# Ranking the first half's router logits token tile by token tile in a hand-planned instruction list

## The chip, the cores and the metric

The kernel runs on one core of one Trainium2 chip. The metric is the device time of one execution in microseconds (us), as the median of several runs. A profile of one execution goes with it: when each instruction ran on each engine, what it waited for, and the clock that was granted to the matrix engine.

The engines are called by their short names: PE multiplies matrices (PEld is its loading of weights, which overlaps the multiplications), DVE is the vector engine, ACT the scalar engine, POOL the general-purpose one and SP the one that issues most DMAs. PE writes to PSUM, which has eight banks; the other engines read results from there.

## The reference, cut to what matters

`x` is 16 batches of 112 tokens of 256 numbers (1,792 tokens), `ctx` is 16 batches of 375. One cross-attention layer and one mixture-of-experts layer follow each other, all in float32:

```python
h = layernorm(x)
q = h @ Wq + bq;  k = ctx @ Wk + bk;  v = ctx @ Wv + bv
x = x + softmax(q @ k.T / 16) @ v                       # per batch

h = layernorm(x)
router_probs = softmax(h @ w_router)                    # 256 -> 8 experts
gate_weights = softmax((h @ w_gating) / 0.1)
expert_out[e] = (silu(h @ w_gate[e]) * (h @ w_up[e])) @ w_down[e]   # 256 -> 1024 -> 256
cw = router_probs * gate_weights
cw = cw / (sum(cw) + 1e-9)
x = x + sum_e expert_out[e] * cw[e]
```

The router logits are the products `h @ w_router` and `h @ w_gating` together: 256 rows to 16 columns.

## The kernel before, in words

The 16 batches make two halves of eight (896 tokens, seven token tiles of 128). The work has two parts.

**The front** does the attention of all 16 batches, the second layer norm, both halves' router logits and the preparation of the first experts' weights. Its instructions are not in program order. Each step is registered with `op(engine, cost, pri, emit, reads, writes, new)`: an engine, a cost that the author wrote down, a rank `pri`, what it reads and writes, and new buffers that it needs. Then `Line.run` (lines 64 to 140) plays the list through with those costs: whenever an engine is free in this play, it takes, of the steps that are ready by then, the one with the lowest rank (line 119). The order that comes out is the order in which each engine gets its instructions. On the chip every engine then works through its own queue in that order and waits wherever something is not ready.

PSUM banks are given out in the same play. A step that opens a result takes one of the eight banks, and the bank is free again when the last step that reads the result is done.

The ranks follow the batch number. For batch `b` the steps on PE are:

| step, name in the profile | line | rank |
|---|---|---|
| two transposes of the context, `ps_cT` (three instructions each) | 1062 | b + 0.1 |
| scores, `ps_sc` | 1074 | b + 0.6 |
| transpose of the softmax, `ps_pp` | 1095 | b |
| softmax times context, `ps_aa` | 1108 | b - 0.4 |
| projection, `ps_po` | 1123 | b |
| transpose of the normalised result, `ps_xx` | 1170 | b - 0.5 |

Between them stand, for each group of four batches, the transposes and projections of the queries (`ps_xT`, line 999, and `ps_qk`, line 1016). After `ps_xx` a copy on ACT or DVE (line 745) puts the batch's columns into `x1T`, which is the input of the router and of the experts.

`route(h)` registers the router of half `h`. `logits(j)` does token tile `j`: two products of a 128 x 128 block of `x1T` with 16 columns, which the profile lists as four instructions of 128 x 16 into `ps_lg` (line 1203). All seven tiles write to one PSUM bank: tile 0 opens it, and each tile is registered as coming after the one before. Tile `j` covers tokens 128 j to 128 j + 127 and so reads two batches of 112 tokens, `b0` and `b1`, which are j and j + 1. One copy on ACT (line 1214) takes all seven tiles out of the bank; the softmax of the router follows on DVE and ACT. For half 0 that chain has no hurry: its last steps have rank 8.7 + 12. The half's splits into high and low parts (lines 297 and 300) do not read the logits.

**The experts** follow: 64 steps of products of the same shape (line 456), with the down projections (line 424) between them, in an order written out in the program. They take the time from about 110 us to the end.

Of the kernel before, what the change touches and what calls it, by code (L numbers as in the profile page):

```python
# [30 lines left out]
class Line:  # L31
# [13 lines left out]
    def op(self, eng, cost, pri, emit, reads=(), writes=(), new=(), waits=(), kb=0, port=False, lands=0.0):  # L45

        n = len(self.ops)
        if not isinstance(eng, tuple):
            eng, cost, go = (eng,), (cost,), emit
            emit = lambda e: go()  # L50
        deps = set()
        for k in reads:
            deps.update(self.writers[k])
        for k in waits:
            deps.update(self.uses[k])
        writes = tuple(writes) + tuple(x[1] for x in new)
        for k in tuple(reads) + writes:
            self.uses.setdefault(k, []).append(n)
        for k in writes:
            self.writers.setdefault(k, []).append(n)  # L60
        self.ops.append((eng, cost, pri, emit, deps, tuple(new), kb, port or eng == ("POOL",), lands))
        return n
# [81 lines left out]
def kernel(  # L144
# [249 lines left out]
    for q in range(E * NJ):  # L394
        e, j = divmod(q, NJ)
# [344 lines left out]
    op = line.op  # L740
# [10 lines left out]
    def bank(key, shape):  # L751

        if key not in banks_of:
            name = "_".join(str(x) for x in key)
            banks_of[key] = psum(line.home[key], f"ps_{name}")
        return shaped(banks_of[key], shape)
# [438 lines left out]
    def route(h):  # L1195

        key = ("lg", h)
        pri = (8.7, 21)[h]
        lg = lgs[h]

        def logits(j):
            for k in range(KC):
                nc.tensor.matmul(  # L1203
                    bank(key, [P, NTT, 2 * E])[:, j, :], x1T[h][:, k, j * P : (j + 1) * P], wr[:, k, :],
                    start=(k == 0), stop=(k == KC - 1),
                )

        for j in range(NTT):
            b0, b1 = j * P // TQ, (j * P + P - 1) // TQ
            op("PE", 0.46, pri, lambda j=j: logits(j),  # L1210
               reads=["wr"] + [("x1T", h * HB + b) for b in range(b0, b1 + 1)] + ([key] if j else []),
               writes=((key,) if j else ()), new=(() if j else (("bank", key, *((("D0", "D1", "D3"),) if h else ())),)))
        op("ACT", 0.26, (pri, 32)[h],
           lambda: nc.scalar.copy(lg, bank(key, [P, NTT, 2 * E]).rearrange("p j (s e) -> p j s e", s=2)),
           reads=(key,), writes=(("l", h),))

        def shift():
            nc.vector.reduce_max(lmx, lg, axis=AX.X)
            nc.vector.tensor_sub(lg, lg, lmx.unsqueeze(3).to_broadcast([P, NTT, 2, E]))

        def shifted(*after):
            op("DVE", 0.9, pri, shift, reads=[("l", h), *after], writes=(("ls", h),))


        def exps():
            nc.scalar.activation(lg[:, :, 0, :], lg[:, :, 0, :], AF.Exp)
            nc.scalar.activation(lg[:, :, 1, :], lg[:, :, 1, :], AF.Exp, scale=10.0)

        if h:
            later_shift.append(shifted)  # L1230
        else:
            shifted()
            op("ACT", 0.5, pri, exps, reads=(("ls", h),), writes=(("le", h), "exp"))

        def sums():
            nc.vector.reduce_sum(lmx, lg, axis=AX.X)
            nc.vector.reciprocal(lmx, lmx)

        def shares():
            nc.vector.tensor_mul(lg, lg, lmx.unsqueeze(3).to_broadcast([P, NTT, 2, E]))  # L1240
            nc.vector.tensor_mul(lpr, lg[:, :, 0, :], lg[:, :, 1, :])

        def rest():
            nc.vector.reduce_sum(lps, lpr, axis=AX.X)
            nc.vector.tensor_scalar_add(lps, lps, 1e-9)
            nc.vector.reciprocal(lps, lps)

        def weights():
            nc.vector.tensor_mul(
                cw[:, h * NTT : (h + 1) * NTT, :], lpr, lps.unsqueeze(2).to_broadcast([P, NTT, E])  # L1250
            )

        if h:
            tail.extend((exps, sums, shares, rest, weights))
            return
        op("DVE", 0.5, pri + 12, sums, reads=(("le", h),), writes=(("w1", h),))
        op("DVE", 0.55, pri + 12, shares, reads=(("w1", h),), writes=(("w2", h),))
        op("DVE", 0.6, pri + 12, rest, reads=(("w2", h),), writes=(("w3", h),))
        op("DVE", 0.3, pri + 12, weights, reads=(("w3", h),), writes=(("cw", h),))
# [5 lines left out]
    early = lambda h: [("x1T", h * HB + b) for b in range(HB // 2)]  # L1265
    late = lambda h: [("x1T", h * HB + b) for b in range(HB // 2, HB)]
    route(0)
    for h in range(NH):
        for i in (X_A11, X_A12):
# [5 lines left out]
    for i in (X_S2, X_S1, X_S3, X_A22, X_S4):  # L1275
        split(0, i, 10.5, *late(0), *([("sx", i)] if i != X_A22 else []))
    route(1)


# [6 lines left out]
    for k in range(EARLY):  # L1286
        pri = 9.5 + k
# [155 lines left out]
```

## Time and profile before

| what | value |
|---|---|
| device time, median of 3 runs | 958.62 us |
| the three runs | 958.07, 958.62, 959.26 us |
| span of the profiled execution, first to last instruction | 958.0 us |
| PE busy in that span | 952.4 us, 99% |
| mean granted PE clock, core 0 | 0.998 |
| the front, to the end of `ps_second` | 0 to about 109.7 us |
| the logits of half 0, first to last matmul | 61.36 to 65.61 us |
| the logits of half 1 | 97.13 to 108.97 us |

Of the profiled execution the page gives the span alone; the timed runs lie 0.1 to 1.3 us above it, and that is taken as what lies around the span together with the spread of the runs.

How to read it: the page lists the busy time of each engine and slices of the span; the chain of waits follows the work that ended last back to the start and names in order of time what it consisted of; the windows view gives busy time, instruction counts and the granted PE clock (1.00 is full) for any stretch. A matmul's end is modelled, so PE can read as busy while it works slowly.

### The profile page before, as it was taken

How to read it: one execution, taken by the hardware profiler on the slowest of the kernel's cores; microseconds unless marked ns; L12 is line 12 of the kernel's file. 1: busy time of each engine (PE TensorE's matmuls, PEld its weight loads, DVE VectorE, ACT ScalarE, POOL GpSimd, SP SyncE). 2: the span in 40 equal slices, each digit the busy share in tenths (PEclk: the TensorE clock that was granted, in tenths of full speed). 3: DMA queues.
4: the chain of work that ended last, by engine and by line, in shares of the span. 5: the costliest groups of instructions: out<-in, count | busy, mean ns of one | idle time of the engine just before them, and what ended most of it. 6: DMA issues, size and time to landing. Idle time of an engine off the chain costs nothing.

```text
span 958.0 us, 16137 instructions
## 1 busy us (share of the span) xinstructions
PE 952.4 (99%) x6076; PEld 896.6 (94%) x6076; DVE 656.1 (68%) x1303; ACT 608.8 (64%) x1236; POOL 377.4 (39%) x481
## 2 busy tenths in 40 slices
PE   9999999999999999999999999999999999999998
PEld 6898999999999999999999999999999999999998
DVE  6878687777576666666575757666666767566675
ACT  5767776666666665666656666666666666666553
POOL 3437973344324433344244332543244431544000
PEclk9999999999999999999999999999999999999999
DMA  9621101011101110011101110111001110100001
GB/s 243 183 58 43 59 23 34 23 34 45 34 12 34 34 45 23 22 36 34 34 23 34 34 34 23 34 34 34 23 23 34 44 34 12 34 23 12 23 17 39
DMA packets 36481, 38.78 MB, mean 40 GB/s; under 512 B 3554, under 2 KB 34404, under 8 KB 36404
## 3 DMA queue, kind: packets, MB, share of 16 engines
q1 hardware_dynamic: 35856, 37.50, 13.2%
q8 instruction: 47, 0.77, 0.3%
q10 hardware_dynamic: 548, 0.27, 0.1%
q14 instruction: 30, 0.25, 0.1%
HBM read 34.08 MB, written 1.84 MB: 37 GB/s over the span
## 4 chain that ended last, share of the span: by engine, by line
PE 98%; DVE 1%; ACT 1%; issue 0%; DVEq 0%; ACTq 0%
PE pd L424 32%; PE pC L456 16%; PE pE L456 16%; PE pA L456 16%; PE pB L456 8%; PE ps_aa L1108 2%; PE ps_sc L1074 2%; PE ps_cT L1062 1%; PE ps_po L1123 1%; PE ps_qk L1016 1%; PE ps_lg L1203 1%; PE ps_pp L1095 1%; PE ps_idle L822 1%; PE ps_xx L1170 0%; PE ps_xT L999 0%; DVE hlo L599 0%
## 5 line engine op out<-in xcount | busy, mean ns | idle before, releaser
L424 PE MATMUL pd<-wd,hhi 128*128 128x256 f32 x1792 | 311.2, 277 | 0.0
L424 PEld LDWEIGHTS pd<-wd,hhi 128*128 128x128 f32 x1792 | 275.8, 188 | 1.9
L424 PE MATMUL pd<-wd,hlo 128*128 128x256 f32 x896 | 248.6, 277 | 0.4 <-DVE hlo L599 0.3
L456 PE MATMUL pC<-xs_hi,w 128*128 128x448 f32 x508 | 185.0, 364 | 0.1
L456 PE MATMUL pE<-xs_hi,w 128*128 128x448 f32 x508 | 184.4, 363 | 0.0
L456 PE MATMUL pA<-xs_hi,w 128*128 128x448 f32 x504 | 183.3, 364 | 0.0
L359 POOL TENSOR_TENSOR w<-raw,w 128x384 fp32r<-128x384 f32 x64 | 78.4, 1225 | 266.0 <-ACT w L349 266.0
L424 PEld LDWEIGHTS pd<-wd,hlo 128*128 128x128 f32 x896 | 168.4, 188 | 0.8 <-DVE hlo L599 0.8
L653 ACT COPY pB<-pA 128x448 f32<-128x448 f32 x122 | 63.8, 523 | 104.0 <-PE pA L456 104.0
L368 POOL TENSOR_TENSOR wd<-rawd,wd 128x512 fp32r<-128x512 f32 x32 | 41.9, 1308 | 182.8 <-ACT wd L366 182.8
L456 PEld LDWEIGHTS pC<-xs_hi,w 128*128 128x128 f32 x508 | 95.3, 188 | 10.9 <-DVE s_90c L678 0.4
L456 PEld LDWEIGHTS pE<-xs_hi,w 128*128 128x128 f32 x508 | 95.4, 188 | 6.6
L456 PEld LDWEIGHTS pA<-xs_hi,w 128*128 128x128 f32 x504 | 94.6, 188 | 5.5
L663 ACT COPY pE<-pB 128x448 f32<-128x448 f32 x122 | 63.1, 517 | 54.2 <-DVE s_6s L530 0.8
L456 PE MATMUL pC<-xs_lo,w 128*128 128x448 f32 x254 | 91.9, 362 | 0.0
L456 PE MATMUL pE<-xs_lo,w 128*128 128x448 f32 x254 | 91.5, 360 | 0.0
L456 PE MATMUL pB<-xs_hi,w 128*128 128x448 f32 x252 | 91.4, 363 | 0.0
L456 PE MATMUL pA<-xs_lo,w 128*128 128x448 f32 x252 | 90.7, 360 | 0.0
L359 POOL TENSOR_TENSOR w<-tt,w 128x512 fp32r<-128x512 f32 x64 | 88.4, 1381 | 0.1
L456 PEld LDWEIGHTS pE<-xs_lo,w 128*128 128x128 f32 x254 | 47.6, 187 | 3.5
L456 PEld LDWEIGHTS pB<-xs_hi,w 128*128 128x128 f32 x252 | 47.3, 188 | 3.1
L456 PEld LDWEIGHTS pC<-xs_lo,w 128*128 128x128 f32 x254 | 47.6, 187 | 2.5
(1456 smaller groups left out, 1786.2 us busy)
## 6 DMA issues: line engine op xcount, KB each, us to landing
raw<-in_L_ffn_w_gate_dram SPq DMA_DIRECT2D x32, 256.0 KB, 2.6
raw<-in_L_ffn_w_up_dram SPq DMA_DIRECT2D x32, 256.0 KB, 2.6
rawd<-in_L_ffn_w_down_dram SPq DMA_DIRECT2D x32, 256.0 KB, 2.6
ctx<-in_ctx_dram SPq DMA_DIRECT2D x13, 336.0 KB
out_dram<-acc SPq DMA_DIRECT2D x6, 256.0 KB, 3.7
wide<-in_ctx_dram SPq DMA_DIRECT2D x3, 336.0 KB, 6.7
wide<-in_x_dram SPq DMA_DIRECT2D x2, 448.0 KB
ctx<-in_ctx_dram SPq DMA_DIRECT2D x13, 39.0 KB
```

The costliest lines, as they stand in the source:

```text
L359: nc.gpsimd.tensor_sub(wts[k][1][:, d], w, f(wts[k][0][:, d]))
L368: nc.gpsimd.tensor_sub(wds[q][1], rawds[q], f(wds[q][0]))
L424: nc.tensor.matmul(pd, hs[a][:, t * P : (t + 1) * P], wds[q][w][:, fi, :], start=(opening and s == 0), stop=(last and s == 2), skip_group_ ...
L456: nc.tensor.matmul(ps, w_[w][:, wi, :], (xs_hi, xs_lo)[a][h][xi], start=(start and s == 0), stop=(stop and s == 2), skip_group_check=True,)
L653: nc.scalar.copy(pb, pa)
L663: nc.scalar.copy(pe, pb)
L822: nc.tensor.matmul(bank(("idle", k), [P, 512]), zero[:, :P], zero, start=True, stop=True)
L1016: nc.tensor.matmul(bank(("qk", g, m, 0), [P, GT]), m_b[k][a][:, m * P : (m + 1) * P], xnT_b[k][w], start=(k == 0 and s == 0), stop=(k == K ...
L1062: nc.tensor.transpose(bank(("cT", b, k), [P, TK])[:, c * KT : (c + 1) * KT], ct()[:, c, k * P : (k + 1) * P], ident[:KT, :KT],)
L1074: nc.tensor.matmul(bank(("sc", b), [TQ, TK]), own(qk_b[k], ("qk", g, k))[:, i * TQ : (i + 1) * TQ], ctT(k), start=(k == 0), stop=(k == KC ...
L1095: nc.tensor.transpose(bank(("pp", b), [KT, NK, TQ])[:, c, :], p()[:, c * KT : (c + 1) * KT], ident[:TQ, :TQ])
L1108: nc.tensor.matmul(bank(("aa", b), [P, KC, TQ])[:, k, :], ct()[:, c, k * P : (k + 1) * P], pT()[:, c, :], start=(c == 0), stop=(c == NK - 1),)
```

## The change

The rank of the seven logits steps of half 0 was 8.7 for all. It becomes 6.5 + 0.5 b1, with b1 = j + 1: 7.0, 7.5, 8.0, 8.5, 9.0, 9.5 and 10.0 for tiles 0 to 6. The second half's logits keep rank 21, and the copy, the softmax and the weights after the logits keep their ranks (8.7 and 20.7). No instruction is added or removed; the list's play gives another order.

```diff
         for j in range(NTT):
             b0, b1 = j * P // TQ, (j * P + P - 1) // TQ
-            op("PE", 0.46, pri, lambda j=j: logits(j),
+            op("PE", 0.46, pri if h else 6.5 + 0.5 * b1, lambda j=j: logits(j),
                reads=["wr"] + [("x1T", h * HB + b) for b in range(b0, b1 + 1)] + ([key] if j else []),
                writes=((key,) if j else ()), new=(() if j else (("bank", key, *((("D0", "D1", "D3"),) if h else ())),)))
```

## The prediction

> **What bounds the kernel now.** I read the page first, then the chain of waits through the front in order of time, then the windows view around the logits with its clock column, then the same windows for the tile `ps_lg` alone, and last PEld's waits. The page:
>
> ```profile
> span 958.0 us, 16137 instructions
> PE 952.4 (99%) x6076; PEld 896.6 (94%) x6076; DVE 656.1 (68%) x1303; ACT 608.8 (64%) x1236; POOL 377.4 (39%) x481
> PE 98%; DVE 1%; ACT 1%; issue 0%; DVEq 0%; ACTq 0%
> ```
>
> PE bounds it: 5.6 us of the span are without a matmul, and the chain is PE's for 98%. The change removes no work. So it can gain only where PE is busy yet slow, and lose only where PE comes to wait. The chain of waits around the logits (start, length, what):
>
> ```profile
> 59.95 1.41 PE ps_aa L1108 x12
> 61.36 0.81 PE ps_lg L1203 x8
> 62.17 0.24 PE ps_xx L1170 x2
> 62.41 0.37 PE ps_lg L1203 x4
> 62.78 0.79 PE ps_po L1123 x6
> 63.57 0.35 PE ps_lg L1203 x4
> 63.92 0.24 PE ps_xx L1170 x2
> 64.16 1.46 PE ps_lg L1203 x12
> 65.61 3.11 PE ps_cT L1062 x15
> 68.72 1.26 PE ps_sc L1074 x4
> ```
>
> Here is such a place. Fifteen transposes take 3.11 us; earlier in the same chain twelve take 1.29 (40.46 to 41.76), so fifteen should take 1.61. The windows view says why. Its columns are stretch, length, busy time of PE, PEld, DVE, ACT and POOL with counts, then the PE clock and the DMA's share:
>
> ```profile
> 61.67:65.08 3.41, 3.41 (x34) 3.41 (x33) 2.68 (x10) 2.22 (x6) 0.55 (x1) 1.00 0.12 36
> 65.08:68.49 3.41, 3.41 (x19) 3.41 (x19) 2.23 (x11) 2.11 (x7) 2.63 (x3) 0.50 0.12 34
> 68.49:71.90 3.41, 3.41 (x18) 2.22 (x17) 2.67 (x7) 2.87 (x9) 1.50 (x2) 1.00 0.00 0
> ```
>
> For 3.41 us the clock was at 0.50, and PE counts as busy throughout. What stood just ahead of it shows in the same view for `ps_lg` alone (columns PE, PEld, ACT, clock):
>
> ```profile
> 61.67:65.08 3.41, 2.63 (x24) 2.63 (x23) 0.00 (x0) 1.00 0.12 36
> 65.08:68.49 3.41, 0.54 (x4) 0.43 (x3) 0.25 (x1) 0.50 0.12 34
> 95.80:99.21 3.41, 0.98 (x8) 0.97 (x8) 0.00 (x0) 1.00 0.09 24
> 99.21:102.63 3.42, 0.51 (x4) 0.53 (x4) 0.00 (x0) 1.00 0.04 10
> 102.63:106.04 3.41, 0.96 (x8) 0.97 (x8) 0.00 (x0) 1.00 0.35 111
> 106.04:109.45 3.41, 1.19 (x8) 1.04 (x8) 0.25 (x1) 1.00 0.42 115
> ```
>
> Logits filled 2.63 us of the stretch before the fall, and a logits matmul streams 16 columns where a transpose streams 125. Half 1 has the same 28 instructions, spread, at most 1.19 us in a stretch, and the clock stayed at 1.00. My reading: a stretch made mostly of logits lets the clock fall, one with a third of them does not.
>
> **What the new order is.** I worked it from ranks and readiness, by hand. Tile j needs the `x1T` of batches j and j+1; the chain has their `ps_xx` at 33.34, 34.77, 40.27, 41.76, 52.52, 56.66, 62.17 and 63.92 us. Tile 0 (rank 7.0) is ready early, but PE has lower ranks until it has done batch 6's transposes (6.1); it goes in at about 41 us, ahead of batch 7's (7.1). Tile 1 (7.5) follows about 1 us later, behind those and `ps_xx` of batch 3. Tile 2 (8.0) waits until attention steps of batches 4 to 7 run out, at about 54. Tiles 3 and 4 (8.5, 9.0) land close together near 60, tile 5 at about 63 and tile 6 at about 65 us, tied to the late `ps_xx`. So at most two tiles, about 0.8 us, stand side by side, with transposes and attention around them.
>
> **The change part by part.**
>
> Gained: the slow stretch. By the clock it costs 3.41 x (1 - 0.50) = 1.71 us. By the rows: the transposes lose 3.11 - 1.61 = 1.50; the last twelve logits took 1.46 where eight took 0.81, so 1.22 at that pace, 0.24 lost; together 1.74. I take 1.71. No wait stands right behind to swallow it: `ps_sc` of batch 9 runs only from 68.72, and what follows it already ran at full clock.
>
> Lost: more changes of shape. The block is four runs of logits; the new order has about six. A tile alone takes 0.35 to 0.44 us (half 1's rows) against 0.40 in the pair of 0.81, so the tiles themselves come out even. What follows a run pays: `ps_po` 0.79 for 0.71, `ps_xx` 0.24 for 0.20, `ps_pp` in half 1 0.41 for 0.32, an expert product 0.70 for 0.60. Two more runs at 0.04 to 0.10 are 0.08 to 0.2; I take 0.15.
>
> New waits of PE: a tile placed right behind the copy into `x1T` can stand for it, and whatever is queued behind it on PE (transposes or scores of the next batch) stands too. Half 1 has two such waits, 0.2 us each (PEld on ACT line 745, 0.4 in all). Tiles 5 and 6 could have them, as tiles in the old block could; 0 to 0.4. On the other side, PEld's waits between 30 and 110 us add up to some 2 us in pieces of 0.2 to 0.5, and another order may drop or add any of them: -0.5 to +0.5. I take 0 for both, since the order from batch 9 on has the same ranks.
>
> The bank: tile 0 now opens the logits' bank at 41 instead of 61 us, the copy at 65.6 still closes it, so one bank of eight is gone for 20 us more. Where a transpose has to wait for a bank, it waits for an eviction, 0.45 to 0.55 us (the copies of `ps_cT`). The list is played with this known, so PE takes another ready step first. Cost 0 to 0.5; I take 0, covered by the transposes of later batches that stand ready.
>
> Moved past: batch 8's context transposes (8.1), at about 42 us so far, now fall behind tile 0 and tile 1 and then behind batches 4 to 7, and so that batch's attention runs some 5 us later. Nobody needs it soon: its `x1T` belongs to half 1, whose logits start at 97. The step issues no DMA. SP's only part is batch 8's rows of `acc`, which the experts first add to at 164.8 us. ACT's copy of the logits, the softmax and the splits wait for tile 6 or batch 7 as before, near 65 us. POOL's next piece, the split at 65.22, waits for batch 7's `x1T`, also unmoved.
>
> Does the gain reach the end? The chain leaves PE at 109.71 for ACT and DVE and comes back at 125.11, but all of it starts from PE's `ps_second`, so it moves along. POOL is busy without a gap from 103.45 to 121.89, preparing weights whose readers come microseconds later (the third step's low part is done at 105.2, read at about 113), and may move less. DVE's slow pieces at 119.17 and 120.82 (1.73 and 1.57 us where others take 0.62) run beside POOL; another phase may lengthen or shorten PE's 0.8 us wait there: +-0.4, taken as 0.
>
> Sum: -1.71 + 0.15 = -1.56 against the profiled execution: a span of 956.4. The timed median is 0.7 above the span, so 958.62 - 1.56 = 957.06, say 957.1 us.
>
> **A rule that speaks against it.** The row: from 65.61 to 68.49 PE did nothing but transposes (the last few logits ahead of them), and at 68.49 the clock was back at 1.00, so here transposes count as activity. The Trainium skill ("TensorE: Matmul & The Clock Gate", Part 4: PE-mode transpose) says they do not count as busy in the same way and do not bring the full clock. By that page tiles 0 and 1 among 2.8 us of transposes near 41 us would make one more idle stretch, and the sum would be -1.56 + 1.71 = +0.15. The trace decides; I keep it as a rival.
>
> **The rivals.**
>
> 1. The timed runs mostly don't have the slow stretch. The profile is one execution, and the runs spread over 1.19 us, which one more or one fewer slow stretch could make. Then only the 0.15 of shape changes is left, or half the gain: 958.3 (957.8 to 958.9). Against it: the last 2.63 us of logits are a fixture of the old order.
>
> 2. It does not do what it says: the clock falls elsewhere, in the transposes near 41 us or around tiles 3 to 6. One slow stretch for another gives 958.8; two, 960.5. Against it: half 1's rows.
>
> 3. Slower: PE runs dry. The transposes are the stock that PE works from while a batch's softmax is on DVE and ACT: from the end of batch 9's scores (69.98) to its `ps_aa` (73.36) it did 15 of them, 1.60 us. If the new order has used that stock up early, PE stands up to 1.60 us per batch. Two batches nearly cancel the gain twice over (+1.64, 960.3); three give +3.24, 961.9, and from 2.2 batches on it is slower by more than 0.2%. For it: batch 8 now runs among batches 9 and 10 and one bank is missing. Against it: that batch's own `ps_aa` and `ps_po` (2.1 us) become filler just there.
>
> **How the numbers follow.** What a measurement of this kernel can tell from no change is about 0.2%, 1.92 us: below 956.70 or above 960.54. My forecast has 0.60, with 956.0 to 957.9 as its own range (gain 0.7 to 2.6 from the waits, the bank and the runs' spread); 0.27 of it lies beyond 956.70. Rival 1 has 0.14, all within 0.2%. Rival 2 has 0.09, 0.03 of it above. Rival 3 has 0.17, above. That makes 0.27 faster, 0.53 the same, 0.20 slower. For 8 in 10 the range goes from 956.0 to 960.0 and leaves out a little of the forecast's low end and most of rival 3.
>
> **What would show it.** Right: no stretch near 65 us at clock 0.50, fifteen transposes anywhere near 1.6 us, at most 1.2 us of `ps_lg` in any 3.41 us, and `ps_second` ending near 108.1 instead of 109.7. Wrong: a 0.50 in the clock column anywhere between 10 and 110 us, PE idle or `ps_aa` rows well above 1.33 us between 60 and 90, or `ps_second` early and the gain lost again by 125 us, at `pd` waiting for DVE.

## The result and the profile after

The change made the kernel slightly slower. The median of 14 runs is 961.6 us (957.8 to 962.8), against 959.0 us (958.1 to 961.4) of 14 runs of the kernel before taken beside them; the ratio is 1.0023 (95% interval 1.0014 to 1.0032). The prediction said 957.1 us, with a range of 956.0 to 960.0: the sign was wrong and the range missed the time.

The page after:

```profile
span 958.0 us, 16124 instructions
PE 948.0 (99%) x6076; PEld 893.6 (93%) x6076; DVE 657.6 (69%) x1301; ACT 609.1 (64%) x1238; POOL 376.8 (39%) x481
PE 96%; DVE 2%; DMA 1%; ACT 0%; issue 0%; SPq 0%; ACTq 0%
```

The span is that of before by chance, but PE has 10.0 us without a matmul instead of 5.6, and PE's share of the chain of waits falls from 98 to 96%. So PE waits more. That its busy time is 4.4 us shorter is no measure of the change: another execution of the kernel before has 947.9 us (`before_again`, below). The play also gave two of DVE's instructions to ACT.

The chain of waits between 42 and 70 us (start, length, what) shows the new order:

```profile
42.26 0.41 PE ps_lg L1203 x4
...
43.61 0.36 PE ps_lg L1203 x4
...
55.94 0.37 PE ps_lg L1203 x4
...
61.28 0.35 PE ps_lg L1203 x4
61.63 1.34 PE ps_sc L1074 x4
62.98 0.35 PE ps_lg L1203 x4
```

Five tiles stand alone among other work; tiles 5 and 6 follow at 64.34 and 66.33. No stretch near 65 us has a clock of 0.50 any more. That part of the plan came out as meant.

What took the gain back is in PE's waits between 20 and 130 us (who waited for whom, total us, times, longest):

```profile
PE ps_po L1123 <- DVE aT L1117: 2.1, 1, 2.1
PE ps_lg L1203 <- ACT wide L745: 0.4, 1, 0.4
PE ps_qk L1016 <- DVE wide L1130: 0.3, 1, 0.3
```

One wait of 2.1 us, in the attention, some 25 us after the last of the moved logits. The timeline of the same kernel around it (start, length, engine, line, result<-inputs, shape; the bracket is the idle time ahead):

```profile
89.80 0.99 POOL L359 TENSOR_TENSOR w<-raw,w 128x384 fp32r<-128x384 f32 x1
90.06 3.13 DVE L1249 TENSOR_TENSOR cw<-lpr,lps 128x56 f32<-128x56 f32 x1
90.76 1.12 POOL L300 TENSOR_TENSOR xs_lo<-wide,xs_hi 128x448 fp32r<-128x448 f32 x1
91.85 1.26 POOL L359 TENSOR_TENSOR w<-tt,w 128x512 fp32r<-128x512 f32 x1
93.11 0.38 DVE L747 CAST aT<-ps_aa 128x224 fp32r<-128x224 f32 x1
93.52 0.39 DVE L1117 TENSOR_TENSOR aT<-ps_aa,aT 128x224 fp32r<-128x224 f32 x1
94.06 0.93 PE L1123 MATMUL ps_po<-wv_b,aT 128*112 128x256 f32 x6 [2.06 <-DVE aT L1117]
```

`cw` is the last step of half 0's router softmax (line 1249, called the weights step below), a product of 56 elements per partition. It starts 0.26 us after POOL has begun the first of three pieces back to back, and ends when the third does. The copy and the low part of `aT` are queued behind it on DVE, and PE needs them for `ps_po`. In the kernel before, the same step met POOL pieces of 0.46 us and cost little:

```profile
86.54 0.46 POOL L335 TENSOR_TENSOR tt<-raw 128x128 f32<-128x128 f32 x1
86.59 0.90 DVE L1249 TENSOR_TENSOR cw<-lpr,lps 128x56 f32<-128x56 f32 x1
86.96 0.46 POOL L336 TENSOR_TENSOR tt<-raw,tt 128x128 f32<-128x128 f32 x1
87.49 0.46 POOL L337 TENSOR_TENSOR tt<-raw,tt 128x128 f32<-128x128 f32 x1
```

There too it stood through the pieces that it met, two of them, and ended as the next one began.

The weights step still has rank 20.7. It moved because moving seven steps of PE re-dealt the whole list, DVE's and POOL's parts of it too.

### The profile page after: what moved, and what is told of

Its sections match the earlier page's. It is cut to its first block, busy times and chain, and to the rows that moved or that the text cites. A ratio compares the mean times of both kernels' runs of the same rounds, so it can differ in the third digit from the quotient of the medians.

```text
span 958.0 us, 16124 instructions
## 1 busy us (share of the span) xinstructions
PE 948.0 (99%) x6076; PEld 893.6 (93%) x6076; DVE 657.6 (69%) x1301; ACT 609.1 (64%) x1238; POOL 376.8 (39%) x481
## 4 chain that ended last, share of the span: by engine, by line
PE 96%; DVE 2%; DMA 1%; ACT 0%; issue 0%; SPq 0%; ACTq 0%
PE pd L424 32%; PE pC L456 16%; PE pE L456 16%; PE pA L456 16%; PE pB L456 8%; PE ps_aa L1108 2%; PE ps_sc L1074 2%; PE ps_po L1123 1%; PE ps_cT L1062 1%; PE ps_qk L1016 1%; DMA wide<-in_x_dram 1%; PE ps_lg L1203 1%; PE ps_pp L1095 1%; DMA wn<-in_L_xattn_Wq_dram 0%; PE ps_xx L1170 0%; DVE cw L1249 0%
```

## The experiments

A kernel's time varies by a few us for reasons outside the change: the part of the profiled span from the third stretch of `pd` to the end took 825.6 to 828.5 us in the profiles below. So beside the timed ratio I measured two segments in each profile: "front", from the first `ps_aa` to the start of `ps_pb`, and "seam", from there to the third stretch of `pd`. The last column says whether the trace has a stretch of 3.41 us at clock 0.50 in the front.

| profile | front, us | seam, us | fall of the clock |
|---|---|---|---|
| before | 85.82 | 19.27 | yes, at 65.08 |
| before, again | 84.37 | 19.25 | no |
| after | 87.36 | 18.52 | no |
| after, again | 87.30 | 18.54 | no |
| after, third | 87.31 | 18.50 | no |
| after, fourth | 88.97 | 18.52 | yes, at 95.30 |
| after, weights step late | 85.08 | 18.55 | no |
| before, weights step late | 85.65 | 19.27 | yes, at 66.44 |
| after, weights step kept off POOL | 84.91 | 18.97 | no |
| the same, last token tile later (`after_port_tail`) | 84.06 | 19.92 | no |
| before, step added ahead of POOL's row (`before_collide`) | 84.46 | 19.26 | no |
| before, step added behind its start (`before_collide2`) | 88.67 | 19.26 | yes, at 95.40 |
| after, step as seven instructions (`after_cw_form`) | 88.01 | 18.52 | no |
| after, step twice (`after_cw_twice`) | 87.52 | 18.53 | no |

**The change again (`after_again`), and the weights step taken out of the front, in both kernels (`after_cw_late`, `before_cw_late`).** The order of all other steps stays as it is:

```diff
-        op("DVE", 0.3, pri + 12, weights, reads=(("w3", h),), writes=(("cw", h),))
+        weights_0.append(weights); op("DVE", 0.3, pri + 12, lambda: None, ...)
...
+        6: weights_0,          # issued in the seventh expert step
```

> The changed kernel itself, unaltered, for a second profile and more runs. Theory A (a vector-engine step that waits for POOL): PE stands about 2 us near 92 us, behind the aT copy that is queued behind the weights step (line 1249), in this profile too, with that step over 2 us long. Theory B (the bank held from 42 us on and the displaced batch 8): PE's waits are spread over 40 to 90 us, and none reaches 1 us. Theory C (the clock falls somewhere else in the typical run): the mean granted clock is 0.998 in most runs and the profile shows one stretch of 3.41 us at 0.50; if it follows the wait of theory A, it begins between 92 and 99 us. Ratio to the kernel before: 1.002.

> The changed kernel with the same order on every engine, except that DVE issues the weights step of half 0 (line 1249) in the seventh expert step, near 140 us, instead of near 90 us. Theory A: the 2.06 us wait of PE at the projection near 92 us goes, and any fall of the clock that followed it; the front ends 1.5 to 2 us earlier, the time falls to 0.9970 to 0.9995 of the kernel before. Theory B: the step was only where the wait showed; the time stays at 1.001 to 1.003. Theory C alone: the clock column still shows 0.50 in most runs, time at 1.001 or above.

> The kernel before with the same edit: its order on every engine, with the weights step of half 0 issued near 140 us. It took 0.90 us there, with 0.2 us of waiting at the projection. Theory A: nothing waited much for it in the old order, so 0.9990 to 1.0002. Theory B: the same. If it gains as much as the other one does, the step is a cost of both orders and not what the change added.

Measured: the change again 962.1 us, ratio 1.0036 (1.0023 to 1.0048), with the same wait of 2.1 us in its profile. With the weights step late the changed kernel takes 959.03, ratio 0.9999 (0.9990 to 1.0008), so the whole loss is gone, though the gain that theory A allowed (0.9970 to 0.9995) is not there; the step itself takes 0.20 us at its new place, and the waits of PE in the same window are

```profile
PE ps_lg L1203 <- ACT wide L745: 0.4, 1, 0.4
PE ps_qk L1016 <- DVE wide L1130: 0.3, 1, 0.3
```

The row of `ps_po` is missing and nothing took its place. In the old order the same edit gains nothing (959.38, ratio 1.0006, 0.9998 to 1.0015; the clock fell in 5 of 11 runs). So it is the meeting of this step with POOL's row that costs, and only in the new order. In the segments: of +2.99 us in the front (87.36 - 84.37, both without a fall) 2.28 are this meeting (87.36 - 85.08) and 0.71 are left for the rest of the new order; the seam gives 0.73 back.

**The step kept off POOL by the list itself (`after_port`).** `op` has a flag by which the play does not put a DVE step beside POOL; some DVE steps carry it, the weights step does not.

```diff
-        op("DVE", 0.3, pri + 12, weights, reads=(("w3", h),), writes=(("cw", h),))
+        op("DVE", 0.3, pri + 12, weights, ..., port=True)
```

> The changed ranks, with the weights step of half 0 marked as one that may not run beside POOL, so that the list keeps the two apart. The order is played anew from there on. Theory A: no vector-engine step over 1 us near 90 us, PE's wait there under 0.5 us, time 0.9970 to 1.0000 of the kernel before. Theory B: 1.001 to 1.003.

Measured: 958.85 us, ratio 0.9995 (0.9986 to 1.0004), with the weights step at 95.2 taking 0.81 us, and no fall of the clock in any of 11 runs. This comes nearest to what the prediction had described, logits spread and no new wait of PE above 0.4 us, and it is level with the kernel before, not faster.

**Single looks at both kernels again (`before_again`, `after_p3`, `after_p4`)**, for whether the clock falls in every execution.

> The kernel before, unaltered, for a profile of an execution in which the clock does not fall (25 of its 31 runs so far had a mean clock of 0.999 or 1.000). Then, from the first ps_aa to ps_pb (85.82 us in the profile shown, 3.41 of them at half clock): theory A with a small cost of the new order itself: 84.0 to 84.5, so that the new order without the wait on the weights step (85.08) is still 0.6 to 1.0 us longer. If it is 85 or more, the new order costs nothing beside that wait.

> The changed kernel, unaltered, for a profile of an execution in which the clock falls (16 of its 23 runs so far had a mean clock of 0.998 or less). Theory A: one stretch of 3.41 us at 0.50 that begins 0 to 4 us after PE's wait of about 2 us behind the weights step, so between 91 and 98 us. Theory C (tiles 0 and 1 among transposes): it begins between 42 and 46 us.

> The same once more, in case the clock does not fall in the other one. Theory A: one stretch at 0.50 beginning between 91 and 98 us, or none; in both the wait at the projection is 1.9 to 2.2 us.

Measured: 955.8 us, and no fall, for before; 958.75 without and 963.0 with a fall for after. So the fall is not a fixture of either kernel. Over all runs whose mean clock is known, before had one in 13 of 72, after in 17 of 25, after with the weights step late or kept off POOL in 0 of 22 (with the last token tile later as well, below, in 1 of 11). A fall costs 85.82 - 84.37 = 1.45 us in before and 88.97 - 87.36 = 1.61 in after.

When the clock falls can be seen because the stretches at 0.50 are all 3.41 us long and stand on a grid. Some microseconds after PE's work has ended the clock drops too. Three profiles have both a fall and this drop: at 65.08 and 959.37 us (before), 66.44 and 957.32 (before, weights step late), 95.40 and 958.97 (`before_collide2`, below). These are 262, 261 and 253 steps of 3.4133 us. So counting back from the drop at the end gives the grid of an execution that had no fall. The logits' share of before_again's grid windows, to be held against the 2.63 us in before's 61.67 to 65.08 (columns PE, PEld, ACT, clock, DMA):

```profile
60.39:63.80 3.41, 1.94 (x16) 2.03 (x16) 0.00 (x0) 1.00 0.24 67
63.80:67.20 3.40, 1.51 (x13) 1.42 (x12) 0.25 (x1) 1.00 0.12 36
```

Here a boundary cut the block in two, and the clock stayed up. The two falls in the old order came after 2.63 us of logits in one window (before, and before with the weights step late); at most 2.05 us in one (`before_collide`, below) and 1.79 (`before_collide2`) gave none there. These are five profiles, and no run changed the block alone; the 22 runs without a fall, with the logits spread, fit it. The same grid explains the falls after the change. The windows view of `after_p4` (PE, PEld, DVE, ACT, POOL, clock):

```profile
91.88:95.30 3.42, 1.35 (x12) 1.23 (x11) 3.39 (x7) 1.64 (x4) 1.28 (x2) 1.00 0.29 81
95.30:98.71 3.41, 3.41 (x8) 2.06 (x7) 2.43 (x10) 1.88 (x6) 2.96 (x4) 0.50 0.13 34
```

and that of the first profile after, where the wait was cut:

```profile
90.14:93.55 3.41, 1.85 (x10) 1.05 (x8) 3.38 (x4) 2.65 (x7) 2.97 (x3) 1.00 0.24 78
93.55:96.97 3.42, 2.91 (x16) 2.37 (x17) 3.32 (x12) 1.44 (x3) 1.27 (x2) 1.00 0.02 5
```

PE busy for 1.35 us of a window was followed by a fall, and so was 1.41 in `before_collide2`; 1.85 here, 1.98 in `after_p3` and 1.74 in `after_cw_form` were not. At the end of the executions, where PE stops, 1.45 us (before, weights step late) was followed by the drop and 1.61 (after, weights step late) was not yet. If the bound is the same there, it lies between 1.45 and 1.61 us busy, that is 1.80 to 1.96 idle. A wait of 2.06 us then does it for at most (3.41 - 2.06 + 2 x (2.06 - 1.80)) / 3.41 = 0.55 of all phases, and for 0.45 with 1.96. 17 of 25 is 0.68. So this estimate from a few profiles gives the falls roughly, and not all of them.

**The loss at the end of the front (`after_port_tail`).** With the wait gone, PE's remaining wait is `ps_lg` of half 1's last token tile, at 112.50, for ACT's copy of batch 15 (the times are those of the first profile after). This kernel is `after_port` with that tile, its copy and the shift issued by the second expert step's script, behind the first stretch of matmuls:

```diff
-        1: """P6 toE w16 P5 p5 P2 exps silu:000 ...
+        1: """P6 toE w16 P5 p5 last P2 exps silu:000 ...
```

> The changed ranks with the weights step kept apart from POOL, and besides the last token tile of half 1, its copy and the first step of its softmax are issued after two products of the second expert step instead of ahead of them, so that PE does not wait there for batch 15 (0.4 us). The same order otherwise. If that wait is what is left of the new order's cost: 0.4 us less than without it, 958.4, ratio to the kernel before 0.9985 to 0.9998. If the second expert step waits for that softmax instead: no gain, 0.9995 to 1.0005.

Measured: 958.69 us, ratio 0.9999 (0.9990 to 1.0008). The front shrank to 84.06 us, the seam grew to 19.92: from `ps_pb` to the first `pd` 12.45 us instead of 11.52. So what the front won, the stretch up to the first `pd` lost; the chain stands there for DVE (`hlo`) in both kernels. Nothing was won.

**The meeting with POOL by itself.** Four kernels. In the old order, an added weights step ahead of the copy of batch 12's `aT` (`before_collide`), or two DVE instructions later, ahead of the copy of batch 13's softmax (`before_collide2`):

```diff
-  lambda e: copy_on(e, aT()[:, 0], ...)
+  lambda e: (extra[0]() if b == 12 else None, copy_on(e, aT()[:, 0], ...))
```

In the new order, the step in another form, seven `tensor_scalar` of 128 x 8 (`after_cw_form`), or twice in a row (`after_cw_twice`):

```diff
-            nc.vector.tensor_mul(cw[...], lpr, lps.unsqueeze(2).to_broadcast(...))
+            for t in range(NTT):
+                nc.vector.tensor_scalar_mul(cw[:, h * NTT + t, :], lpr[:, t, :], lps[:, t : t + 1])
```

> The kernel before with its own order, and one thing added: DVE issues the weights step of half 0 a second time, directly ahead of its copy of batch 12's result (line 747, at 89.98 us in the profile shown), where POOL has three pieces in a row (90.44 to 93.78). The logits stay in their block. Theory A (what costs is such a step meeting POOL's row with PE's projection queued behind it): the added step takes 2 to 3.8 us instead of 0.2, PE waits 1.5 to 3.4 us at the projection, ratio 1.0015 to 1.0045, and the clock falls in more of the runs than in the kernel before. Theory B (the new ranks, the bank and the displaced batch cost): only its 0.2 us, ratio 0.9995 to 1.0008.

> The kernel before with its own order and its block of logits, and the added weights step two DVE instructions later than in the other try: after batch 12's low part (line 1117) and directly ahead of the copy of batch 13's softmax (line 747, 90.70 us in the profile shown), so that it starts after POOL's row has begun at 90.44. PE needs that copy for ps_aa of batch 13 at 92.05. Theory A: the added step takes 2.5 to 3.4 us and ends with POOL's row near 93.8; PE waits 1.5 to 2.8 us at ps_aa; from the first ps_aa to ps_pb 86 to 87.2 us instead of 84.4; the clock falls in more runs; ratio 1.0015 to 1.004. Theory B: 0.2 us, ratio 0.9995 to 1.0008.

> The changed kernel with its own order, but the weights step written as seven products of 128 x 8 elements with one number per partition, in place of one product of two 128 x 56 tensors. Theory A, if the wait belongs to the form with two tensors from SBUF: the seven take 0.06 to 0.15 us each, no wait over 0.5 us at the projection, ratio 0.9990 to 1.0008. If any form waits for POOL's row: seven that end near 93 us, PE's wait again 2 us, ratio 1.002 to 1.004. Theory B: 1.002 to 1.004.

> The changed kernel with the weights step issued twice in a row. If the step waits for POOL's row to end (theory A), the second runs after that row and takes 0.2 us: PE's wait 2.2 to 2.4 us. If the step is slow at that place by itself, the second takes 3 us as well: PE's wait about 5 us.

The first was a miss: 959.35 us, ratio 1.0001 (0.9992 to 1.0009), with no fall in 11 runs. Its timeline shows why:

```profile
89.98 0.21 DVE L1250 TENSOR_TENSOR cw<-lpr,lps 128x56 f32<-128x56 f32 x1
90.57 1.00 POOL L359 TENSOR_TENSOR w<-raw,w 128x384 fp32r<-128x384 f32 x1
```

The added step came 0.59 us before POOL's row and took 0.21. A little later, in `before_collide2`, it came 0.26 us after the row had begun:

```profile
90.04 1.00 POOL L359 TENSOR_TENSOR w<-raw,w 128x384 fp32r<-128x384 f32 x1
90.30 3.12 DVE L1250 TENSOR_TENSOR cw<-lpr,lps 128x56 f32<-128x56 f32 x1
93.99 0.38 PE L1170 MATMUL ps_xx<-ident,x1n 112*128 112x112 f32 x2 [2.54 <-DVE total L1102]
```

One instruction of 0.21 us, put at this place, makes PE wait 2.54 us for a DVE step queued behind it, and the kernel 964.25 us, ratio 1.0054 (1.0042 to 1.0066), with a fall of the clock in 5 of 6 runs. That is more than the 1.0015 to 1.004 expected; its front is 2.85 us longer than that of the kernel before with a fall (85.82). So the effect is made in the kernel before, without any of the change. Two steps in a row took 3.38 us together, so the second cost 0.25, and PE waited 2.3 us (961.4 us, one run): the stand is paid once, by whoever comes first. The seven `tensor_scalar` took 3.88 us, the first 3.07 and the others 0.22 each (962.1 us, ratio 1.0044, 1.0031 to 1.0058): that form stands as well. In all four kernels with the stand the step ends 0.02 to 0.08 us after the third POOL piece. The falls of `after_cw_form`, 2 of 5 runs with a wait of 2.8 us, are fewer than the estimate above would give (0.67 to 0.77).

The Trainium skill ("SBUF — State Buffer", Who interferes with whom) has a rule for this: DVE and POOL share a pair of SBUF ports that whoever starts first holds for its whole instruction, and a DVE instruction with two inputs in SBUF contends with a POOL instruction that reads SBUF; "Issue order, not op shape, decides who blocks." The runs agree: 0.21 us ahead of the row, 3.12 behind its start. These runs add that DVE did not get in between three POOL instructions that followed each other without a gap.

## Why the prediction was wrong, by its own steps

**The new order by hand: right.** The seven tiles stand at 42.26, 43.61, 55.94, 61.28, 62.98, 64.34 and 66.33 us where I had put them at about 41, 42, 54, twice near 60, 63 and 65; only tiles 3 and 4 are not side by side.

**"Gained: the slow stretch", -1.71: right as the price of a fall, wrong as a term of the median.** In no profile after the change does the clock fall near the logits of half 0. But a fall costs 1.45 us, and only 13 of 72 executions of the old kernel had one, so that the gain in a typical run is near nothing, and 0.3 us in the mean (1.45 x 13 / 72). So this step failed first: without the loss below the time would still have been level. This is the prediction's first rival. I argued against it that the block of logits is a fixture of the old order. It is, but whether it fills a window of the clock's grid depends on where the grid lies in that execution, and one profile cannot show that. `after_port` measures what was left: no falls, and 0.9995 of the time before.

**"The timed median is 0.7 above the span": wrong, and a hint that I passed by.** The difference that I used is 958.62 - 958.0 = 0.62, and it compares one execution's span with the median of others. In 72 runs of the kernel before that have both numbers the time lies 1.65 to 1.79 us above the run's own span (955.82 and 954.1 in `before_again`). A span of 958.0 therefore meant about 959.7 us, above all three timed runs: the profiled execution was one of the slower ones, which is what the first rival said.

**"New waits of PE" and "Moved past", taken as 0: the step that failed and turned no gain into a loss.** I priced the waits of the moved logits themselves, and wrote that ACT's copy, the softmax and the splits go "as before, near 65 us". Their ranks did, their places did not: the weights step went from 86.59 to 90.06 us, into POOL's row. The trace of before held the row needed: 0.90 us for a step of 56 elements per partition beside POOL's pieces of 0.46, with 0.20 us for the reciprocal just ahead of it. I did not ask what that step would cost beside longer pieces. Its price in the new order is 2.28 us without a fall, and some 0.68 x 1.61 = 1.1 us more in the mean through the clock.

**"Does the gain reach the end?", +-0.4 taken as 0:** the seam became 0.73 us shorter (19.25 to 18.52), more than I allowed for, and in favour of the change.

**"More changes of shape", +0.15:** not measured by itself. The half's seven tiles take 2.62 us in the chain after and 2.79 in that of `before_again`, so the tiles did not become dearer; what the steps behind them pay lies in the 0.71 us below.

**The rivals.** The third named PE running dry, and PE does stand, but for a stalled copy, once, for 2.06 us, and not batch after batch for want of transposes. The second named a fall elsewhere, near the logits: there was none there; the falls after the change follow the new wait. By the rule of the Trainium skill that I weighed ("TensorE: Matmul & The Clock Gate", Part 4: PE-mode transpose), the tiles among transposes near 42 us should have let the clock fall; in no profile of the new order did it fall there.

**The sum as it measured.** Without falls: +2.28 for the meeting, +0.71 for the rest of the new order in the front, -0.73 in the seam, together +2.26. With falls in 0.68 instead of 0.18 of the executions, at 1.61 and 1.45 us: +1.09 - 0.26, together +3.1 in the mean. The two timed comparisons gave ratios of 1.0023 and 1.0036, that is +2.2 and +3.5 us. Split by the mean clock, the timed runs give less: without a fall 960.29 against 958.81 us (medians of 8 and 58 runs), that is +1.5, so +2.26 from single profiles is not exact. Not settled: of the +0.71, half (0.4 us) is the wait of half 1's last logits for ACT, which shows as a new row above; for the rest there are only small shifts (`ps_qk` waiting 0.3 us for DVE), not tested one by one. The time outside the span, 2.0 us in the mean of the runs after against 1.7, was not looked into either.

## What to carry to other kernels

When a list scheduler deals the order, a new rank for one step moves others that were not touched; look at the neighbours on every engine for a pair that interferes and that the scheduler does not know of, here a short DVE step and a row of POOL pieces. A short step that took several times its normal length in the old trace is the warning, and the cheapest remedy is to tell the scheduler (`port=True`) or to move the step out of the busy part. A gain read from one profiled execution is a gain of the median only if most executions have what is to be removed, so compare that execution's own time with the others first.

## What the runs showed of the hardware

A DVE product of 0.20 us stood for 3.13 us, through three POOL instructions without a gap between them; in the old order, among pieces of 0.46 us, it stood for 0.90 only. In that row the view shows a gap of 0.07 us (87.42 to 87.49) after the second piece, where the step ended. Whether such a gap is what lets DVE in was not tested. Not every POOL instruction holds DVE off: in `before_collide` the step took 0.21 us while a 112x1 POOL instruction (line 1153) is shown from 89.55 to 90.59.

The falls fit a grid of 3.4133 us whose place in the program differs from one execution to the next, so that the same program in the same order has them in some executions and not in others. A window need not be idle for it: PE busy 1.35 of 3.42 us was enough, and so was a window in which PE counts as fully busy, 2.63 us of it with matmuls of 16 columns.
